# Five gated-state buffers instead of four, and output-projection weights that are loaded once for each sequence

## The chip, the cores and the metric

The kernel runs on one core of a Trainium2 chip. The metric is the device time of one execution in microseconds (us). Engines are named as in the profile: PE (TensorE), with PEld for its weight loads, DVE (VectorE), ACT (ScalarE), POOL (GpSimd) and SP (SyncE, which issues most DMAs). Each engine works through its own queue in order, and waits on semaphores for the others.

## The reference

The input is 16 sequences of 512 rows of 256 numbers, float32. A first layer is a Mamba block that scans in both directions, a second one is a soft mixture of experts; each ends with a sum and a layer norm.

```python
# layer 1, for each sequence
xf, res = split(x @ in_proj_w.T)                  # 512 channels each
xf = silu(causal_conv(xf));  xb = silu(causal_conv_b(xf))
delta = softplus(dt_proj(x_proj(xf)));  B, C = x_proj(xf)[...]   # 16 states
dA = delta * A;  dBu = delta * u * B              # for each channel, row and state
y = sum over states of C * (decayed running sum of dBu)  + u * D
y = (y_forward + y_backward) * silu(res)
x = layernorm(x + y @ out_proj_w.T)
# layer 2
x2 = layernorm(x) * gain + shift
logits = x2 @ slot_embeds.T                       # 16 experts x 64 slots
slots = softmax over rows(logits).T @ x2
e_out = (gelu(slots @ Wg + bg) * (slots @ Wu + bu)) @ Wd + bd
x = layernorm(x + softmax over slots(logits) @ e_out)
```

## The kernel before

**The scan.** For each of the 16 sequences `scan_part` runs four times: forward and backward for channels 0 to 255 (two chunks of 128), then both for channels 256 to 511. One call goes over the 16 states in pairs, and for each pair over its two chunks. A pair of states of one chunk is called a unit here: 64 units for each sequence, 1024 in all. What one unit does, with the lines of before:

- SP loads the rows of B and C for the pair, spread over all partitions, into `bs` (L431) and `cs` (L432), three buffers each, and sometimes a block of diagonals `dg` (L435).
- POOL makes `db`, the inputs of the recurrence, as `du` times `bs` (L442; 128x1024, three buffers).
- ACT makes the decay with an Exp, into the PSUM bank in which the scan will run (L459; three banks), and the gate `th` with a Tanh (L461; three buffers).
- DVE runs the recurrence (L465 forward, L467 backward; 128x512, twice in a unit) and multiplies it with the gate, (th + 1) * h, into one half of `hg` (L470, twice in a unit). `hg` is 128x1024, 4 KB for each partition, and has four buffers.
- POOL multiplies `hg` with `cs` in place (L471).
- PE adds `hg` up in the PSUM bank `acc`, by transposing it block by block against the identity (L386, eight matmuls of 128x128 for a unit). Only then is the `hg` buffer free.

For some states the product of L442 is made on PE instead, with diagonals, as `hd` (L420); its scan runs in that bank.

The matmuls of L386 are not issued with their unit. A unit is put on a list, and the list is worked off to a depth of two:

```python
pending.append((r == n == 0, n == 0, r == 1 and n == NS - 2, c, hg, accs, w, v["u"], f"acc_{q}_{c}", done))
evict()
...
beside_scan()
...
add_up(2)
```

So the sums of unit i stand in PE's queue behind what was issued beside units i + 1 and i + 2.

**The work beside it.** Everything else is written as generators that yield at places where they would wait: `prep` (input projections, convolutions, time steps for the next part), `front` (`finish`: output projection, norm, and then `dispatch`: logits and slots) and `back` (`experts` and `combine`, from sequence 3 on after each second one). `beside_scan` lets each give one piece after each unit. Instructions marked `late` keep their place in the program's order; for the others the builder's scheduler sets the order on each engine, by its own idea of times and of free buffers.

**finish and its weights.** `constants` loads the output projection's weights `outT` once, 128 x 4 x 256 float32, and halves them on DVE (L181, L182). `finish(b, y)` loads x again (L115), transposes y (L640), copies the transposed bank to `yt` on ACT (L645), multiplies with `outT` (L651, `po`), adds x (L660), norms, stores, makes the normed rows `xn`, and turns them into `x2T` (L691), one buffer of 4 KB for each partition. `x2T` goes to DRAM (L696) and is read by `dispatch` in the logits' matmuls (L710). `finish` of one sequence begins beside the first units of the next one, when `dispatch` of the sequence before has been drained.

**The end.** After the last scan the last sequence's `finish` and the last pair's experts and combine run with wider buffers.

Of the kernel before, what the change touches and what calls it, by code (L numbers as in the profile page):

```python
# [9 lines left out]
F32 = mybir.dt.float32  # L10
BF16 = mybir.dt.bfloat16
AF = mybir.ActivationFunctionType
ALU = mybir.AluOpType
# [4 lines left out]
P = 128  # L18
L = 512
NL = L // P  # L20
DM = 256
NM = DM // P
DI = 512
ND = DI // P
# [31 lines left out]
def seq_layers(tc, ident, neghalf, a, out):  # L56
# [22 lines left out]
    with ExitStack() as ctx:  # L79
# [47 lines left out]
        def late(ins):  # L127

            return tc.keep_in_program_order(ins)
# [45 lines left out]
        def constants():  # L175
            blanks(1)
            steps(side[0], "f", "")
            projections(side[1], "b", "_b")
            steps(side[1], "b", "_b")
            outT = const.tile([P, ND, DM], F32, name="outT")  # L180
            nc.sync.dma_start(outT, a["out_projT"].rearrange("(c p) o -> p c o", p=P))  # L181
            late(nc.vector.tensor_scalar(outT, outT, 0.5, None, ALU.mult))  # L182
            return outT

        projections(side[0], "f", "")
        blank = p2.tile([P, 4 * DM], F32, tag="W", name="blank", bufs=3)
# [220 lines left out]
        def scan_part(b, r, p, v, accs, done, then):  # L407
# [17 lines left out]
            for n in range(0, NS, 2):  # L425
                q = f"{b}_{r}_{p}_{n}"
                k = 1 if n + 1 in ds else 2

                bs = p4.tile([P, 2, L], F32, tag="bs", name=f"bs_{q}")
                cs = p4.tile([P, 2, L], F32, tag="cs", name=f"cs_{q}")  # L430
                nc.sync.dma_start(bs[:, :k, :], v["bc"][0, n : n + k, :].unsqueeze(0).to_broadcast([P, k, L]))  # L431
                nc.sync.dma_start(cs, v["bc"][1, n : n + 2, :].unsqueeze(0).to_broadcast([P, 2, L]))  # L432
                if n + 3 in ds:
                    dg = p4.tile([P, L], F32, tag="dg", name=f"dg_{q}", bufs=1)
                    nc.sync.dma_start(  # L435
                        dg.rearrange("p (l s) -> p l s", l=NL),
                        diag_dram[r, ds.index(n + 3), :, : P * P].rearrange("l (p s) -> p l s", p=P),
                    )
                for c in chunks:
                    dt, rr, du = v[c][:3]  # L440
                    db = p4.tile([P, 2, L], F32, tag="db", name=f"db_{q}_{c}")
                    nc.gpsimd.tensor_tensor(  # L442
                        db[:, :k, :], du.unsqueeze(1).to_broadcast([P, k, L]), bs[:, :k, :], ALU.mult
                    )
                    hg = p4.tile([P, 2, L], F32, tag="hg", name=f"hg_{q}_{c}", bufs=4)
                    hs = {}
                    for j in range(2):
                        if j < k:
                            dec = h = ps_h.tile([P, L], F32, tag="h", name=f"h_{q}_{c}_{j}")
                            hs[j] = (h, dec, db[:, j, :])  # L450
                        else:
                            h = made.pop((n + j, c))
                            dec = p4.tile([P, L], F32, tag="dec", name=f"dec_{q}_{c}", bufs=2)
                            hs[j] = (h, dec, h)

                    ths = {}
                    for j in range(2) if k == 2 else (1, 0):
                        s = slice(n + j, n + j + 1)
                        nc.scalar.activation(hs[j][1], dt, AF.Exp, scale=w["A"][:, c, s])  # L459
                        ths[j] = p4.tile([P, L], F32, tag="th", name=f"th_{q}_{c}_{j}")  # L460
                        nc.scalar.activation(ths[j], rr, AF.Tanh, bias=LN_1E12 / 2, scale=w["Ah"][:, c, s])  # L461
                    for j in range(2):
                        (h, dec, add), th = hs[j], ths[j]
                        if r == 0:
                            nc.vector.tensor_tensor_scan(h, dec, add, 0.0, ALU.mult, ALU.add)  # L465
                        else:
                            nc.vector.tensor_tensor_scan(  # L467
                                h[:, ::-1], dec[:, ::-1], add[:, ::-1], 0.0, ALU.mult, ALU.add
                            )
                        nc.vector.scalar_tensor_tensor(hg[:, j, :], th, 1.0, h, ALU.add, ALU.mult)  # L470
                    nc.gpsimd.tensor_tensor(hg, hg, cs, ALU.mult)  # L471
                    pending.append(
                        (r == n == 0, n == 0, r == 1 and n == NS - 2, c, hg, accs, w, v["u"], f"acc_{q}_{c}", done)
                    )
                    evict()

                    nxt_n = n if c == chunks[0] else n + 2
                    if nxt_n + 1 in ds:
                        for x in sides:
                            x.take_up()  # L480
                        by_diagonal(nxt_n + 1, chunks[1] if c == chunks[0] else chunks[0])
                    beside_scan()
                    if k == 1:
                        diags.pop(0)
                    add_up(2)
# [145 lines left out]
        def finish(b, y):  # L631

            xt = load_x(b)
            for h in range(NL // 2):
                yts = []
                for lc in (2 * h, 2 * h + 1):
                    yield 1
                    pt = bank(f"pyt_{b}_{lc}")
                    for c in range(ND):
                        nc.tensor.transpose(  # L640
                            pt[:, c * P : (c + 1) * P], y[:, c, lc * P : (lc + 1) * P], ident
                        )
                    yield HOLD
                    yt = p2.tile([P, L], F32, tag="fr", name=f"yt_{b}_{lc}")
                    late(nc.scalar.copy(yt, pt))  # L645
                    yts.append(yt)
                yield GAP + 1
                po = bank(f"po_{b}_{h}")
                for i, yt in enumerate(yts):
                    for c in range(ND):  # L650
                        nc.tensor.matmul(  # L651
                            po[:, i * DM : (i + 1) * DM],
                            yt[:, c * P : (c + 1) * P],
                            outT[:, c, :],
                            start=(c == 0),
                            stop=(c == ND - 1),
                        )
                yield HOLD
                x2 = xt[:, 2 * h : 2 * h + 2, :].rearrange("p c d -> p (c d)")
                late(nc.vector.tensor_tensor(x2, x2, po, ALU.add))  # L660
            mv = row_moments(nc, p2, xt, "m1", late)
            yield WAIT
            rs, sh = factors(mv, "m1")

            r2 = p2.tile([P, NL], F32, tag="m1_r2", name=f"m1_r2_{b}")
            nc.gpsimd.tensor_tensor(r2, mv[:, :, 1], rs, ALU.mult)
            nc.gpsimd.tensor_tensor(r2, r2, rs, ALU.mult)
            nc.gpsimd.tensor_scalar(r2, r2, EPS, None, ALU.add)
            nc.gpsimd.tensor_tensor(r2, r2, neghalf[:, :NL], ALU.pow)
            yield WAIT  # L670
            yield WAIT
            scaled(xt, xt, sh, rs)
            nc.scalar.dma_start(x1_dram[b].rearrange("(c p) d -> p c d", p=P), xt)
            yield 0
            xn = p1.tile([P, NL, DM], F32, tag="xn", name=f"xn_{b}")
            for i in range(NL):
                ins = nc.scalar.activation(xn[:, i, :], xt[:, i, :], AF.Identity, scale=r2[:, i : i + 1])
                if i == 0:
                    late(ins)
            yield WAIT  # L680
            x2T = p1.tile([P, NM, L], F32, tag="x2T", name=f"x2T_{b}")
            for k in range(NM):
                yield GAP + 1
                pt = bank(f"px2_{b}_{k}")
                for lc in range(NL):
                    nc.tensor.transpose(
                        pt[:, lc * P : (lc + 1) * P], xn[:, lc, k * P : (k + 1) * P], ident
                    )
                yield HOLD
                late(  # L690
                    nc.scalar.activation(  # L691
                        x2T[:, k, :], pt, AF.Identity, bias=shift[:, k : k + 1], scale=gain[:, k : k + 1]
                    )
                )
            if not wide:
                nc.scalar.dma_start(x2_dram[b].rearrange("k p l -> p k l"), x2T)  # L696
            yield from dispatch(b, xn, x2T)
# [341 lines left out]
        fwd = {}  # L1039
        prep.add(1, prep_forward(0, 0, ND, fwd))  # L1040
        prep.drain()
        outT = constants()
        prep.add(1, prep_pair(0, 0, 0, fwd))
        prep.drain()
        for w, s in zip(side, "fb"):
# [101 lines left out]
```

## Time and profile before

| | before |
|---|---|
| median of 3 runs | 5327.67 us (5324.82 to 5328.87) |
| the profiled execution | 5322.25 us, span 5320.5 us |
| PE busy | 4310.4 us (81%) |
| DVE busy | 4560.6 us (86%) |
| ACT busy | 4104.9 us (77%) |
| POOL busy | 4681.6 us (88%) |
| granted TensorE clock | 0.897 |
| DMA | 907.82 MB, mean 171 GB/s |

Busy time is the time in which an engine ran instructions of the program; the span is from the first to the last. A group in the profile is one kind of instruction: line, engine, operation, the tiles written and read, shapes and count; behind the bar its busy time, the mean of one in ns, and the engine's idle time just before these instructions with what ended most of it. A row of waits names who waited, for whom, total us, times and the longest.

### The profile page before, as it was taken

The numbers are of one execution on the slowest core, as the hardware profiler recorded it, in microseconds if no ns is written. First come the engines' busy times: TensorE is split into PE (matmuls) and PEld (weight loads), VectorE is DVE, ScalarE is ACT, GpSimd is POOL, SyncE is SP. The second block draws the span as 40 slices with busy tenths as digits, with TensorE's granted clock in tenths as the row PEclk, the third lists the DMA queues.
The fourth block names the chain that finished last, engine by engine and source line by source line (L and its number), as shares of the span: only waits on it lengthen the run. The fifth ranks groups of instructions, "written<-read, shape, count | busy, mean of one in ns | idle before, by whom it ended". The sixth has DMA issues, their size and how long they took to land. (4 is left out here: it accounts for less than half of the span.)

```text
span 5320.5 us, 74550 instructions
## 1 busy us (share of the span) xinstructions
PE 4310.4 (81%) x24498; PEld 3411.1 (64%) x24498; DVE 4560.6 (86%) x6284; ACT 4104.9 (77%) x6573; POOL 4681.6 (88%) x2537
## 2 busy tenths in 40 slices
PE   5677776897778978788788878889787897878889
PEld 3556565676567756676666766667666676657667
DVE  7999999889998899888898888988898889987733
ACT  6777878887888877888887887888778887777644
POOL 6999999989999899999999989998999989988710
PEclk7778888998899989999899988899888998889999
DMA  5444444675446644576446754467544664447545
GB/s 141 137 129 152 126 142 131 211 234 152 146 146 224 222 144 143 171 226 206 132 140 198 236 169 151 134 210 230 157 151 144 217 227 149 144 153 230 168 135 168
DMA packets 614820, 907.82 MB, mean 171 GB/s; under 512 B 84606, under 2 KB 404734, under 8 KB 614432
## 3 DMA queue, kind: packets, MB, share of 16 engines
q1 hardware_dynamic: 532740, 859.35, 50.9%
q10 hardware_dynamic: 81692, 43.70, 3.1%
q8 instruction: 195, 3.19, 0.2%
q14 instruction: 193, 1.58, 0.1%
HBM read 840.34 MB, written 62.56 MB: 170 GB/s over the span
## 5 line engine op out<-in xcount | busy, mean ns | idle before, releaser
L471 POOL TENSOR_TENSOR hg<-hg,cs 128x1024 f32<-128x1024 f32 x1024 | 2416.9, 2364 | 125.0 <-DVE hg L470 108.0
L442 POOL TENSOR_TENSOR db<-du,bs 128x1024 f32<-128x1024 f32 (+1 forms) x1024 | 2087.7, 2042 | 227.8 <-DVE h L465 84.1
L470 DVE SCALAR_TENSOR_TENSOR hg<-th,h 128x512 f32<-128x512 f32 x1744 | 1156.8, 679 | 183.4 <-PE acc L386 105.9
L386 PE MATMUL acc<-ident,hg 128*128 128x128 f32 x8192 | 1163.6, 292 | 106.4 <-POOL hg L471 84.6
L386 PEld LDWEIGHTS acc<-ident,hg 128*128 128x128 f32 x8192 | 1034.4, 152 | 284.6 <-POOL hg L471 131.3
L467 DVE TENSOR_TENSOR_SCAN h<-h,db 128x512 f32<-128x512 f32 x872 | 1044.9, 1219 | 104.9 <-ACT h L459 92.6
L465 DVE TENSOR_TENSOR_SCAN h<-h,db 128x512 f32<-128x512 f32 x872 | 1044.1, 1219 | 44.5 <-ACT h L459 43.6
L461 ACT ACTIVATE th<-rr,Ah_f 128x512 f32<-128x512 f32 x1024 | 724.6, 714 | 200.9 <-DVE hg L470 198.1
L461 ACT ACTIVATE th<-rr,Ah_b 128x512 f32<-128x512 f32 x1024 | 721.3, 712 | 153.5 <-DVE hg L470 143.5
L459 ACT ACTIVATE h<-dt,A_f 128x512 f32<-128x512 f32 x872 | 591.4, 680 | 99.5 <-DVE hg L470 96.3
L459 ACT ACTIVATE h<-dt,A_b 128x512 f32<-128x512 f32 x872 | 592.3, 680 | 85.6 <-DVE hg L470 81.7
L420 PE MATMUL hd<-dg,duT 128*128 128x128 f32 x2432 | 375.7, 305 | 73.2 <-ACT duT L364 27.1
L420 PEld LDWEIGHTS hd<-dg,duT 128*128 128x128 f32 x2432 | 347.9, 220 | 84.5 <-ACT duT L364 29.5
L710 PE MATMUL pl<-x2T,seT 128*128 128x512 f32 x512 | 294.1, 704 | 78.4 <-DVE hg L470 37.4
L838 PE MATMUL peo<-Wd,ht 128*128 128x256 f32 x1024 | 258.1, 408 | 63.2 <-DVE rr L346 36.6
L869 PEld LDWEIGHTS pg<-st,Wg 128*128 128x128 f32 x2048 | 243.1, 195 | 94.1 <-issue 82.8
L811 PE MATMUL pu<-st,Wu 128*128 128x128 f32 x2048 | 255.6, 284 | 49.3 <-DMA Wu<-in_Wu_dram 27.0
L1015 PE MATMUL cpo<-ceo,ct 128*128 128x256 f32 x1024 | 256.0, 407 | 43.2 <-DVE rr L346 40.0
L811 PEld LDWEIGHTS pu<-st,Wu 128*128 128x128 f32 x2048 | 245.9, 199 | 60.6 <-DVE h L467 29.5
L838 PEld LDWEIGHTS peo<-Wd,ht 128*128 128x128 f32 x1024 | 205.5, 206 | 106.1 <-DVE rr L346 39.2
L869 PE MATMUL pg<-st,Wg 128*128 128x128 f32 x2048 | 265.0, 284 | 4.5 <-DMA st<-s_dram 3.4
L1015 PEld LDWEIGHTS cpo<-ceo,ct 128*128 128x128 f32 x1024 | 207.2, 207 | 87.2 <-DVE rr L346 42.7
(165 smaller groups left out, 6754.0 us busy)
## 6 DMA issues: line engine op xcount, KB each, us to landing
cs<-bc SPq DMA_DIRECT2D x512, 512.0 KB, 3.9
bs<-bc SPq DMA_DIRECT2D x360, 512.0 KB, 5.2
Wg<-in_Wg_dram SPq DMA_DIRECT2D x128, 512.0 KB, 5.7
Wu<-in_Wu_dram SPq DMA_DIRECT2D x128, 512.0 KB, 5.8
Wd<-in_Wd_dram SPq DMA_DIRECT2D x128, 512.0 KB, 5.5
dg<-diag_dram SPq DMA_DIRECT2D x152, 256.0 KB, 4.3
bs<-bc SPq DMA_DIRECT2D x152, 256.0 KB, 3.5
x<-in_x_dram SPq DMA_DIRECT2D x32, 512.0 KB, 6.5
```

The lines of the kernel that those rows point to most:

```text
L386: ins = nc.tensor.matmul(accs[c][:, s], hc[:, j, s], ident, is_transpose=True, start=False, stop=(last and j == 1 and lc == NL - 1),)
L420: ins = nc.tensor.matmul(h[:, s], v[c][3][:, s], dg[:, s], start=True, stop=True)
L442: nc.gpsimd.tensor_tensor(db[:, :k, :], du.unsqueeze(1).to_broadcast([P, k, L]), bs[:, :k, :], ALU.mult)
L459: nc.scalar.activation(hs[j][1], dt, AF.Exp, scale=w["A"][:, c, s])
L461: nc.scalar.activation(ths[j], rr, AF.Tanh, bias=LN_1E12 / 2, scale=w["Ah"][:, c, s])
L465: nc.vector.tensor_tensor_scan(h, dec, add, 0.0, ALU.mult, ALU.add)
L467: nc.vector.tensor_tensor_scan(h[:, ::-1], dec[:, ::-1], add[:, ::-1], 0.0, ALU.mult, ALU.add)
L470: nc.vector.scalar_tensor_tensor(hg[:, j, :], th, 1.0, h, ALU.add, ALU.mult)
L471: nc.gpsimd.tensor_tensor(hg, hg, cs, ALU.mult)
L811: nc.tensor.matmul(pu[:, fc * P : (fc + 1) * P], got["Wu", e][:, k, fc * P : (fc + 1) * P], st[:, k, :, j * SL : (j + 1) * SL], start=(k = ...
L838: nc.tensor.matmul(po[:, j * DM : (j + 1) * DM], ht[:, fc, :], got["Wd", e0 + j][:, fc, :], start=(fc == 0), stop=(fc == NF - 1),)
L869: nc.tensor.matmul(pg[:, fc * P : (fc + 1) * P], got["Wg", e][:, k, fc * P : (fc + 1) * P], st[:, k, :, j * SL : (j + 1) * SL], start=(not ...
```

## The change

`hg` gets a fifth buffer. To make room, `outT` is no longer a constant of its own: each `finish` loads it again, into the buffer of `x2T`, which is of the same size. There it takes the place of the sequence before's turned rows, and it is overwritten by its own sequence's. The weights come unhalved, so the factor 0.5 moves into the eviction of the transposed y: the copy becomes an Identity activation with a scale of 0.5.

```diff
@@ constants()
-            outT = const.tile([P, ND, DM], F32, name="outT")
-            nc.sync.dma_start(outT, a["out_projT"].rearrange("(c p) o -> p c o", p=P))
-            late(nc.vector.tensor_scalar(outT, outT, 0.5, None, ALU.mult))
-            return outT
@@ scan_part
-                    hg = p4.tile([P, 2, L], F32, tag="hg", name=f"hg_{q}_{c}", bufs=4)
+                    hg = p4.tile([P, 2, L], F32, tag="hg", name=f"hg_{q}_{c}", bufs=5)
@@ finish(b, y)
             xt = load_x(b)
+            outT = p1.tile([P, ND, DM], F32, tag="x2T", name=f"outT_{b}")
+            nc.sync.dma_start(outT, a["out_projT"].rearrange("(c p) o -> p c o", p=P))
             for h in range(NL // 2):
...
-                    late(nc.scalar.copy(yt, pt))
+                    late(nc.scalar.activation(yt, pt, AF.Identity, scale=0.5))
@@ at the start
-        outT = constants()
+        constants()
```

## The prediction

> **What bounds the kernel now.** I first cut the span at 46 and 5080 us, the first `db` product and the last scan product, and asked for busy time in the two stretches.
>
> ```profile
> core 0: us, PE busy (x) PEld busy (x) DVE busy (x) ACT busy (x) POOL busy (x), PEclk, DMA share, GB/s
> 46.00:5080.00 5034.00, 4071.57 (x23243) 3225.50 (x23244) 4472.82 (x6051) 3993.91 (x6345) 4662.82 (x2478) 0.89 0.54 171
> ```
>
> The scans take 5034 of 5320.5 us. POOL works 4662.8 of them, 92.6%, and is idle 371; DVE works 88.9%. The other 240 us after 5080 have no `hg` in them. So POOL is the nearest to a bound, and the change can win at most its 371 idle us. The costliest groups show what POOL does:
>
> ```profile
> L471 POOL TENSOR_TENSOR hg<-hg,cs 128x1024 f32<-128x1024 f32 x1024 | 2416.9, 2364 | 125.0 <-DVE hg L470 108.0
> L442 POOL TENSOR_TENSOR db<-du,bs 128x1024 f32<-128x1024 f32 (+1 forms) x1024 | 2087.7, 2042 | 227.8 <-DVE h L465 84.1
> ```
>
> Each unit costs POOL 2.36 + 2.04 = 4.4 us, and what it waits for, when it waits, is DVE. Next, who DVE waits for, from the list of waits (total us, times, longest):
>
> ```profile
> ACT th L461 <- DVE hg L470: 341.6, 310, 3.2
> ...
> POOL hg L471 <- DVE hg L470: 108.0, 59, 7.8
> DVE hg L470 <- PE acc L386: 105.9, 89, 4.8
> ...
> DVE hd L467 <- PE hd L420: 40.6, 42, 1.9
> ...
> DVE hg L470 <- ACT th L461: 39.4, 33, 4.5
> ```
>
> The third line is the one that the change aims at: a gate (L470) wants a new `hg`, and the matmuls at L386 that read its old content four units ago have not run. 89 times, never over 4.8 us, about one unit's time (5034 us / 1024 units = 4.9 us). The timeline shows why they are late, and who pays:
>
> ```profile
> 3096.43 2.05 PE L869 MATMUL pg<-st,Wg 128*128 128x128 f32 x16
> ...
> 3098.32 1.04 PE L386 MATMUL acc<-ident,hg 128*128 128x128 f32 x8
> ...
> 3099.39 1.29 DVE L470 SCALAR_TENSOR_TENSOR hg<-th,h 128x512 f32<-128x512 f32 x2 [2.37 <-PE acc L386]
> ...
> 3100.82 2.35 POOL L471 TENSOR_TENSOR hg<-hg,cs 128x1024 f32<-128x1024 f32 x1 [2.61 <-DVE hg L470]
> ```
>
> L386 stands behind an expert's matmuls in PE's queue; DVE loses 2.37 us and POOL, which wants this very `hg` next, 2.61. At 85 of the 89 waits the gate was of the unit that POOL takes next: there is no store to live on.
>
> **Part 1: the fifth `hg`.** With five buffers a gate needs the matmuls of five units ago, one unit (4.9 us) earlier than now. The longest wait is 4.8 us, so all 105.9 us should go from DVE. What of it comes back in the span is another question. I went along the timeline and took, for each of the 89 waits, POOL's idle time within its next four instructions, at most the wait itself. Sequence 9 (of 0 to 15) as an example (wait, counted): 2.31, 1.69; 1.16, 0.93; 0.77, 0.77; 0.18, 0; 0.97, 0.97; 1.73, 0; 1.42, 0.69; 1.38, 1.38; 0.18, 0.18; 2.37, 2.37; 0.38, 0: 9.0 of 12.8 us. Over all sequences 71.2 of 105.9, a share of 0.67. Odd sequences from 3 to 13 hold most (7.2 to 9.0 each), the last has 15.6, the even ones from 4 on nothing.
>
> What is late next is PE itself: its queue is unchanged, and the diagonal product (L420) stands in it too. DVE waits for `hd` within 15 us behind these waits; taking each at most at the wait before it, that is 27.4 us. A DVE that comes earlier waits there again: 27.4 x 0.67 = 18.4 us are lost. 71.2 - 18.4 = 52.8 us of gain. Bounds: 0 (all comes back as another wait) to 105.9 (all of it is on the path). I take 52.8, from the waits themselves.
>
> **Part 2: the order.** Set side by side, the two programs have the same order on PE but for one transpose; about 1165 of DVE's 6285 instructions and 1080 of ACT's 6481 stand elsewhere, since the builder's order went by four buffers. 280 gates that had two or more instructions between them and their scan now have at most one; 147 went the other way. On POOL all but some 180 are in place. Gates nearer to their scans give POOL its input earlier, which is in my favour; but they may come before their `th`. Bounds: a gain of the 108 us that POOL waits for gates, most of them counted above already, and a loss of the 64 us worked out for the first rival below. I take 0, as the moves go both ways. ACT gets 351 table loads in place of 346, since five more pairs of the experts' Gelu are split by an Exp or Tanh. The groups have them at 1283 ns: 6.4 us of ACT, which is idle 1040 us of the scan stretch, but the loads stand in just the places where DVE is short. Bounds 0 to 6.4; I take 6.4.
>
> The page "ScalarE: Activation LUTs" of the Trainium skill, section "What ACT_TABLE_LOAD costs", speaks harder against this: a switch costs the load and a drain, together 2.66 us. By it this item would be an estimated 13.3 us. The trace shows no such drain: at 3058.89 a load of 1.28 us follows 0.02 us after an activation's end, and the next activation starts at 3060.19.
>
> **Part 3: the weights, once for each sequence.** Removed at the start: one DVE multiplication of 0.689 us at 38 us, while the first scan waits for its decay; 0. Added: 15 more DMAs of 0.5 MB (7.9 MB on 907.82), each 0.506 us to issue on SP, 7.6 us of SP in all, and 3.7 us to land. Each stands in SP's order near the second or third `bs` load of the next sequence and waits for the last L710 of the sequence before, which read `x2T`. SP at the place, in the timeline of before:
>
> ```profile
> 2773.55 0.32 SPq L431 DMA_DIRECT2D bs<-bc  x1
> 2783.65 0.32 SPq L432 DMA_DIRECT2D cs<-bc  x1
> 2785.96 0.32 SPq L431 DMA_DIRECT2D bs<-bc  x1
> 2786.37 0.39 SPq L435 DMA_DIRECT2D dg<-diag_dram  x1
> ```
>
> The last L710 before it ended at 2783.3. So the new load goes out at about 2783.7, and the `bs` and `dg` loads behind it, which went at 2786.0 and 2786.4, keep their time. They have more cover: from a `bs` issue to the product that reads it pass 22 us in the median, and 5.2 of those are the landing; from this `dg` to its matmul pass 24.2. `po`, the first reader of the weights, starts at 2839.6. The last sequence's load waits for an L710 that ended at 5049.4, and `po` starts at 5095.1. All hidden: 0. If the cover were gone, 15 x (0.506 + 3.7) = 63 us is the most the loads themselves could cost. The halving moves into the eviction (L645): a copy of 581 ns becomes an Identity with a constant scale. The nearest row is L274, PSUM in, 128x512, constant scale: 580 ns; the dearest is L691 with two per-row operands, 768. 64 x 0 to 64 x 0.187 = 0 to 12 us of ACT; I take 0, for L274.
>
> A rule that speaks against more loading is in "SBUF — State Buffer", section "A bandwidth-pool intuition that's wrong (but worth ruling out)": "HBM is almost always your end-to-end bottleneck". Were it so here, 7.9 MB at 170 GB/s would add an estimated 46 us and nearly undo the gain. The profile has the DMA engines at a share of 0.54 in the scan stretch, so no.
>
> **Sum.** 52.8 - 6.4 = 46 us. The profiled execution took 5322.25 us (span 5320.5), 0.1% under the median of 5327.67; I take the 46 us off the median: 5281 us, 0.9% faster. This case has its own range of 5222 (all 106 us) to 5317.
>
> **Rivals.**
> *The tanh takes the place of the buffer (slower).* Gates now stand nearer to their scans, so they may come before their `th`. Net 280 - 147 = 133 gates; each can wait for at most one Tanh, 0.714 us (L461): 95 us of DVE, by the same share of 0.67, 64 us. Against the gain of 46 that is 18 us slower, 5346. It decides from 46 / (0.714 x 0.67) = 96 of the 133 gates. For it: DVE waits for `th` already, 39.4 us. Against it: only 33 times, though 401 gates follow their scan directly today, and ACT waits 341.6 us for DVE to free a `th`, so ACT is mostly early.
> *PE is the bound at these places (no change).* The fifth buffer is there but the next thing from PE (`hd`, `pl`, `pz`) comes no earlier. For it: PE's queue has the same order and is 81% busy, and 27.4 us of `hd` waits do follow. Against: 62 us in all on `hd`, against 106. Time: 5328 - 0 to 10.
> *SP is blocked (slower).* If L710 is later in the changed run, `bs`, `cs` and `dg` stand behind the weights' load. It costs nothing until the delay is over some 15 us; then each us counts in 15 places, 5 us too many make 75, and with the gain 5357. Against: the margin above.
>
> **How the numbers follow.** Forecast 0.68; tanh 0.16; PE 0.10; SP 0.06. The three runs of before lie within 0.08%, so I call anything within 0.2% (10.7 us) no change. The PE case and a little of the neighbours make 0.10 of no change; tanh and SP make 0.22 slower. The range goes from 5222, the full 106 us, to 5350, just over the tanh case. SP's case and a gain beyond 106 through the better order stay outside.
>
> **What would show it.** The wait of L470 on L386 should fall from 106 us to under 10, POOL's idle time in the scan stretch from 371 to about 325, and its L471 waits on L470 from 108 to about 70. Waits of DVE on `hd` should grow from 62 towards 80. Wrong if the wait of L470 on `th` goes from 39 to near 100 (tanh), if L386's wait goes but POOL's idle stays at 371 (PE), or if POOL waits for the landing of `bs` (SP).

## The result, and the profile after

The changed kernel is slower: 5362.94 us (5356.56 to 5378.82) against 5327.72, ratio 1.0071 with an interval of 1.0047 to 1.0096. The profiled execution took 5368.21 us, span 5366.4, at a granted clock of 0.894 (before 0.897). Before was timed anew beside each batch of the experiments, with medians from 5327.5 to 5329.3 us. Times are medians of fast runs; one of the eleven runs of `rows_moved` came in the slower state (5423.51 us) and is left out. The scans end at 5124 us in place of 5080; the tail is 242.6 us, before 240.4. The lines of this kernel up to `finish` stand four lower than before: the gate is L466, the product of POOL L467, `db` L438, the scans L461 and L463, Exp L455, Tanh L457, the sums L382, `hd` L416, the scaled rows of a norm L621.

The scan stretch, and the two groups of POOL:

```profile
core 0: us, PE busy (x) PEld busy (x) DVE busy (x) ACT busy (x) POOL busy (x), PEclk, DMA share, GB/s
46.00:5130.00 5084.00, 4106.05 (x23269) 3241.34 (x23270) 4459.40 (x6051) 4000.20 (x6349) 4660.31 (x2478) 0.89 0.54 171
```

```profile
L467 POOL TENSOR_TENSOR hg<-hg,cs 128x1024 f32<-128x1024 f32 x1024 | 2414.5, 2361 | 112.6 <-DVE hg L466 44.0
L438 POOL TENSOR_TENSOR db<-du,bs 128x1024 f32<-128x1024 f32 (+1 forms) x1024 | 2084.8, 2039 | 284.0 <-issue 114.0
```

POOL doesn't work longer than before: 4660 us in the stretch, before 4663. DVE and ACT are within 15 us of before; PE, at the slightly lower clock, is busy 4341.6 us of the whole execution, before 4310.4. The difference on POOL is idle time; taken from 44.6 to 5123.8 us it goes from 371 to 417. `hg` waits less for its input (125.0 to 112.6), `db` more (227.8 to 284.0); 44 of these 56 us stand under "issue" (70.2 to 114.0), for which the profile names no releaser. The list of waits says for what (total us, times, longest):

```profile
ACT th L457 <- DVE hg L466: 359.9, 348, 8.5
...
DVE h L463 <- ACT h L455: 125.2, 57, 5.9
...
ACT x L621 <- POOL m_sh L616: 85.1, 16, 7.7
...
DVE hg L466 <- PE acc L382: 77.1, 45, 6.1
...
DVE hg L466 <- ACT th L457: 46.5, 41, 6.0
...
POOL hg L467 <- DVE hg L466: 44.0, 42, 6.4
```

The gate's wait for the sums, at which the buffer aimed, is 77.1 us and not gone (before 105.9). At each of its 45 places the missing sum is that of the unit five before, where it was four before: VectorE now runs one unit further ahead and finds the fifth buffer taken too. The scans wait longer for the Exp (backward 92.6 to 125.2), and a wait that was at 42.6 us has doubled: ScalarE's scaled rows of the output norm, for POOL's factors. The timeline shows one such place, in sequence 8:

```profile
2587.61 0.60 ACT L621 ACTIVATE x<-x,m_sh,m_rs 128x256 f32<-128x256 f32 x1 [7.68 <-POOL m_sh L616]
...
2588.12 0.67 ACT L455 ACTIVATE h<-dt,A_b 128x512 f32<-128x512 f32 x1
...
2588.82 1.23 DVE L463 TENSOR_TENSOR_SCAN h<-h,db 128x512 f32<-128x512 f32 x1 [5.86 <-ACT h L455]
...
2589.36 6.77 PE L1015 MATMUL cpo<-ceo,ct 128*128 128x256 f32 x16 [6.22 <-ACT duT L360]
...
2596.17 0.48 DVE L1024 SCALAR_TENSOR_TENSOR cx<-cpo,csm,cx 128x256 f32<-128x256 f32 x1 [4.94 <-PE cpo L1015]
...
2600.47 2.36 POOL L438 TENSOR_TENSOR db<-du,bs 128x1024 f32<-128x1024 f32 x1 [5.43 <-DVE h L463]
```

Only the first row of a norm is `late`; the other three are free, and the builder has put one of them in front of Exps and copies. ScalarE stands at it for 7.68 us, and what is queued behind it is late: an Exp, for which the scan waits 5.86 us, and two copies of `duT`, for which TensorE waits 6.22 us before it makes `cpo` (a product of `combine`). VectorE then waits 4.94 us for `cpo`, the scans behind that are late too, and POOL, which needs a buffer that a scan reads, pays 5.43. Before, the copies ran ahead of the rows, and the four rows ran together at this place, with next to no wait:

```profile
2578.41 2.08 ACT L625 ACTIVATE x<-x,m_sh,m_rs 128x256 f32<-128x256 f32 x4 [0.45 <-POOL m_sh L620]
```

In after one row stands five places ahead of the next in twelve sequences (2 to 13); in before two or three places in eight of the sixteen.

### The profile page after: what moved, and what is told of

Same layout as the page of the kernel before. It is cut to its first block, busy times and chain, and to the rows that moved or that the text cites. A ratio compares the mean times of both kernels' runs of the same rounds, so it can differ in the third digit from the quotient of the medians.

```text
span 5366.4 us, 74363 instructions
## 1 busy us (share of the span) xinstructions
PE 4341.6 (81%) x24498; PEld 3422.9 (64%) x24498; DVE 4548.0 (85%) x6283; ACT 4111.5 (77%) x6578; POOL 4680.4 (87%) x2537
## 4 chain that ended last, share of the span: by engine, by line
DVE 38%; PE 28%; ACT 16%; issue 11%; POOL 5%; DMA 2%; SPq 0%; DVEq 0%; ACTq 0%; POOLq 0%
DVE h L463 10%; DVE hg L466 9%; DVE h L461 9%; PE acc L382 4%; ACT th L457 4%; ACT h L455 3%; PE peo L838 3%; PE pl L710 2%; PE pg L869 2%; PE cpo L1015 2%; PE px L287 2%; POOL db L438 2%; POOL hg L467 2%; PE pq L746 2%; PE hd L416 2%
## 5 line engine op out<-in xcount | busy, mean ns | idle before, releaser
L467 POOL TENSOR_TENSOR hg<-hg,cs 128x1024 f32<-128x1024 f32 x1024 | 2414.5, 2361 | 112.6 <-DVE hg L466 44.0
L438 POOL TENSOR_TENSOR db<-du,bs 128x1024 f32<-128x1024 f32 (+1 forms) x1024 | 2084.8, 2039 | 284.0 <-issue 114.0
L466 DVE SCALAR_TENSOR_TENSOR hg<-th,h 128x512 f32<-128x512 f32 x1744 | 1155.7, 677 | 164.5 <-PE acc L382 77.1
L382 PE MATMUL acc<-ident,hg 128*128 128x128 f32 x8192 | 1164.5, 292 | 119.8 <-POOL hg L467 96.4
L382 PEld LDWEIGHTS acc<-ident,hg 128*128 128x128 f32 x8192 | 1033.6, 152 | 298.1 <-POOL hg L467 130.2
L463 DVE TENSOR_TENSOR_SCAN h<-h,db 128x512 f32<-128x512 f32 x872 | 1044.3, 1218 | 134.2 <-ACT h L455 125.2
L461 DVE TENSOR_TENSOR_SCAN h<-h,db 128x512 f32<-128x512 f32 x872 | 1046.7, 1218 | 66.5 <-ACT h L455 60.6
L457 ACT ACTIVATE th<-rr,Ah_f 128x512 f32<-128x512 f32 x1024 | 724.1, 714 | 219.5 <-DVE hg L466 216.7
L457 ACT ACTIVATE th<-rr,Ah_b 128x512 f32<-128x512 f32 x1024 | 723.4, 712 | 146.9 <-DVE hg L466 143.2
L455 ACT ACTIVATE h<-dt,A_f 128x512 f32<-128x512 f32 x872 | 592.0, 681 | 110.1 <-DVE hg L466 104.0
L455 ACT ACTIVATE h<-dt,A_b 128x512 f32<-128x512 f32 x872 | 591.2, 679 | 77.7 <-DVE hg L466 75.1
L416 PE MATMUL hd<-dg,duT 128*128 128x128 f32 x2432 | 368.3, 301 | 64.0 <-ACT duT L360 29.5
L416 PEld LDWEIGHTS hd<-dg,duT 128*128 128x128 f32 x2432 | 338.3, 215 | 75.8 <-ACT duT L360 31.6
L1015 PE MATMUL cpo<-ceo,ct 128*128 128x256 f32 x1024 | 264.2, 417 | 79.3 <-DVE rr L342 39.4
L869 PEld LDWEIGHTS pg<-st,Wg 128*128 128x128 f32 x2048 | 256.7, 204 | 98.1 <-issue 82.8
L869 PE MATMUL pg<-st,Wg 128*128 128x128 f32 x2048 | 278.9, 293 | 5.3 <-DMA st<-s_dram 3.5
```

Of the source, the lines that this page charges most:

```text
L382: ins = nc.tensor.matmul(accs[c][:, s], hc[:, j, s], ident, is_transpose=True, start=False, stop=(last and j == 1 and lc == NL - 1),)
L416: ins = nc.tensor.matmul(h[:, s], v[c][3][:, s], dg[:, s], start=True, stop=True)
L438: nc.gpsimd.tensor_tensor(db[:, :k, :], du.unsqueeze(1).to_broadcast([P, k, L]), bs[:, :k, :], ALU.mult)
L463: nc.vector.tensor_tensor_scan(h[:, ::-1], dec[:, ::-1], add[:, ::-1], 0.0, ALU.mult, ALU.add)
L869: nc.tensor.matmul(pg[:, fc * P : (fc + 1) * P], got["Wg", e][:, k, fc * P : (fc + 1) * P], st[:, k, :, j * SL : (j + 1) * SL], start=(not ...
L1015: nc.tensor.matmul(po[:, :DM], cts[sc // 4][:, sc % 4 * P : (sc % 4 + 1) * P], eos[sc // 4][:, sc % 4, :], start=(sc == 0), stop=(sc == NS ...
```

## The experiments

Orders are held with edges between neighbours on an engine that carry no semaphore; the matmuls, data and buffers stay as they are (shortened here):

```python
for engine, steps in want.items():        # the other program's order
    for i in steps:
        tc.add_manual_dep(i, prev.name, NoSync, reason="order"); prev = i
```

**1. The three parts of the change: weights, buffer, order.** `weights_only` has four buffers:

```diff
-  hg = p4.tile([P, 2, L], F32, tag="hg", name=f"hg_{q}_{c}", bufs=5)
+  hg = p4.tile([P, 2, L], F32, tag="hg", name=f"hg_{q}_{c}", bufs=4)
```

> The weights' part of the change alone: they are loaded for each sequence and halved in the eviction, with four gated-state buffers; the order on PE, DVE, POOL is that of before (DVE within 4 of 6285 instructions). Theory A (the fifth buffer is good by itself, but the builder's order, which counts with it, puts waiting instructions in front of the scan's on ACT, DVE and POOL): the weights cost nothing, 5323 to 5333 us. Theory B (the reload through SP's queue and the new activation are the loss): 5350 to 5365 us. Theory C (the fifth buffer is of no use, PE sets the pace at those places, and the new order is the whole loss): 5323 to 5333 us as in A.

5333.09 us, ratio 1.0012 (1.0003 to 1.0021). `five_old_order` has five, with the order of before held on all five engines:

> The whole change, but with the order of before pinned on all five engines (the 16 loads of the weights stand free on SP). Theory A: the gain of the prediction appears, 5270 to 5300 us, and the wait of the gates for the sums falls from 106 to under 20 us. Theory B: the gain less the loss by the reload, 5310 to 5340 us. Theory C: 5322 to 5334 us, the waits for the sums turned into others.

5324.68 us, ratio 0.9993 (0.9984 to 1.0002). So the weights cost 5.6 us, the buffer under one order gives 8.4, and the builder's new order costs 5362.9 - 5324.7 = 38 us. By the spread of the runs I estimate that the first two are good to some 3 us, and every difference from after to some 10, as its four runs lie 22 us apart. The granted clock doesn't explain the 38: the run of after at 0.899 took 5357.68 us, those of `five_old_order` at 0.898 from 5315.89 to 5326.81. `five_old_order` lies in theory C's range and not in A's, and as C says, the waits for the sums turned into others. The buffer does what it says: in `five_old_order` no wait of the gate for the sums is left in the list (95.5 us in `weights_only`). What the list has in its place:

```profile
DVE h L463 <- ACT h L455: 128.0, 97, 3.4
...
DVE hd L463 <- PE hd L416: 58.0, 49, 4.4
DVE hg L466 <- ACT th L457: 56.6, 41, 6.0
...
DVE h L461 <- ACT h L455: 44.1, 32, 3.5
DVE hd L461 <- PE hd L416: 39.5, 26, 4.6
```

Against `weights_only` the Exp's waits are up by 24 us (147.7 to 172.1), those for `hd` by 42 (55.1 to 97.5), for Tanh by 12 (44.8 to 56.6): 78.6 of 95.5 us came back on the same engine.

**2. Which engine's order.** The same kernel with ScalarE's order alone held, and with VectorE's alone:

> The whole change with the order of before pinned on ACT alone; the builder then leaves DVE within 600 and POOL within 70 instructions of the order of before. Theory A, if ACT's early norm (the scaled rows that wait 7.7 us for POOL ahead of the scan's Exp) is the main loss: 5280 to 5325 us, and the wait of the scaled rows for POOL falls from 85 to about 43 us. If DVE's order is: 5340 to 5365 us. Theory B: 5345 to 5365 us. Theory C: 5328 to 5350 us.

> The whole change with the order of before pinned on DVE alone; POOL and PE then come out as before, and ACT within 50 instructions, with 12 more table loads than before (15 us of ACT). Theory A: 5280 to 5315 us. Theory B: 5325 to 5355 us. Theory C: 5328 to 5343 us.

5360.82 (1.0048 to 1.0073) and 5353.99 us (1.0039 to 1.0064). Neither mends it: they are 36 and 29 us above `five_old_order`. With ScalarE's order held the even sequences from 4 on no longer lose, but the odd ones do, 3 to 7 us each; with VectorE's held, the builder splits more pairs of Gelus (358 table loads), and most odd sequences lose 3 to 5 us. One engine's order without the others' is no repair. In `five_old_act` ScalarE has the rows and the 346 table loads of before, so what is wrong with ScalarE's order in after isn't needed for a loss of this size.

**3. The early rows.** One line, so that no scaled row can leave its place:

```diff
-                if i == 0:
-                    late(ins)
+                late(ins)
```

> The changed kernel with one line moved: all four scaled rows of a norm are kept in program order on ScalarE, and not the first alone, so that no row can be put ahead of the Exps and copies of the scan. The weights and the five buffers stay. Theory (the new order loses where a scaled row that the builder put early waits for GpSimd's norm factors with ScalarE's queue behind it): the 4.1 us that each even sequence loses at unit 19 goes, 25 us over six even sequences, 12 more table loads or fewer make no difference, so 5363 - 25 = 5338 us (5330 to 5346), and ScalarE's wait for the norm factors falls from 85 us in 16 waits to under 50. The odd sequences keep their 3.5 to 5 us each. Rival (the new order is worse everywhere, and this place is only where a lag that is already there shows): the loss goes to the next wait, 5355 to 5370 us, with the even sequences still behind by 4 to 6 us each.

5297.48 us, ratio 0.9939 (0.9925 to 0.9952): 65 us off, more than either theory gave. But this builds a new order, with some 400 of VectorE's instructions elsewhere, so the row was then moved alone, in after and in before, all else held:

> The changed kernel with its own order held on all five engines, and twelve instructions of ScalarE moved: in sequences 2 to 13 the one scaled row of the output norm that stands four instructions ahead of the others is put right before them. Nothing else moves, and the 351 table loads stay. Theory (most of the loss is this one row, since with all rows kept in order the kernel takes 5297 us): 12 rows that wait some 5 us each with ScalarE's queue behind them are about 50 us, so 5363 - 50 = 5313 us (5300 to 5330), and ScalarE's wait for the norm factors falls from 85 to under 50 us. Rival (the row costs only the 4.1 us of unit 19 in even sequences, and the rest of that kernel's gain came from the other instructions that moved with it, 400 of VectorE's 6285 and twelve table loads less): 5363 - 25 = 5338 us (5332 to 5345).

> The kernel before with its order held on all five engines, and the first scaled row of the output norm put next to the second in the eight sequences in which it stands two or three places ahead (in the others it stands in its place). Theory (before pays for the row in each second sequence, 3.6 us at unit 19 in six of them, and after in both kinds): 5328 - 22 = 5306 us, 5298 to 5312; then after's early rows cost 29 us against 22, and only 7 of the 35 us between the kernels are theirs. Rival (before's row is free, and its 31 us came from the hundred other instructions that moved): 5322 to 5330 us; then all 29 us of after's rows are new.

After: 5332.35 us (ratio to before 1.0007, 0.9998 to 1.0016), 31 us for twelve rows, which is just in the rival's range. Before: 5310.21 us, ratio 0.9969 (0.9959 to 0.9979), 19 us for eight, as its theory says. So before paid for its early rows as well, at unit 19 of its odd sequences, and only 12 of the 35 us between the two kernels are theirs. The line itself, in before and with four buffers:

> The kernel before, four buffers and its weights loaded once, with all scaled rows of a norm kept in program order. Theory (before, too, waits for the norm factors, 64.8 and 42.6 us, but without much behind it, as its row stands two or three places ahead and not five): 5329 us, 5318 to 5332, no difference. Rival (the line is worth its 65 us with four buffers too, and the fifth buffer has no part in it): 5265 to 5300 us.

> The changed kernel with four buffers and all scaled rows in program order: beside the run with five it gives what the fifth buffer is worth once the early row is gone. Theory (weights cost 5 us, the buffer is worth about 35 us with an order in which no row waits): 5334 us, 5322 to 5338. Rival (the rows' order is the gain, with any number of buffers): within 8 us of the 5297 us with five.

5297.49 (0.9932 to 0.9958) and 5298.47 us (0.993 to 0.9958). The rivals of both held: the 31 us have nothing to do with the fifth buffer, and beside 5297.48 for five the buffer is worth 1 us once the builder orders for itself. Weights loaded sixteen times cost 1.0 us here. Neither of these can be told from zero: five runs each lie 10 to 16 us apart. The line also holds the rows of `combine`'s norm, whose wait for their factors falls from 64.8 to 48.6 us in before; what that part gives alone wasn't tried.

**4. A pair that the new order splits.** One pass of `experts` has 16 Gelus, one for each expert, in pairs; such a pass is called a group of Gelus here. In after, ScalarE's seventh and eighth Gelu of a group have an Exp between them:

```profile
2968.30 1.28 ACT L892 ACT_TABLE_LOAD   x1
2969.59 0.60 ACT L892 ACTIVATE ht<-pg 128x512 f32<-128x512 f32 x1
...
2970.82 1.28 ACT L455 ACT_TABLE_LOAD   x1
2972.11 0.69 ACT L455 ACTIVATE h<-dt,A_f 128x512 f32<-128x512 f32 x1
...
2972.82 1.28 ACT L895 ACT_TABLE_LOAD   x1
2974.12 0.60 ACT L895 ACTIVATE ht<-pg 128x512 f32<-128x512 f32 x1
...
2975.82 1.28 ACT L455 ACT_TABLE_LOAD   x1
2977.11 0.69 ACT L455 ACTIVATE h<-dt,A_f 128x512 f32<-128x512 f32 x1
```

Before, the same two stand together behind one load:

```profile
2961.99 0.60 ACT L892 ACTIVATE ht<-pg 128x512 f32<-128x512 f32 x1
2962.48 0.59 ACT L895 ACTIVATE ht<-pg 128x512 f32<-128x512 f32 x1
```

Four loads, of which two go when the pair stands together. With the rows moved and these six pairs joined (351 loads become 339):

> The run with twelve rows moved (5334 us), and beside that the experts' seventh and eighth Gelu, which the new order alone has apart with an Exp between them, put together in six groups: 12 table loads of 1.28 us less, nothing else moved. Theory (what is left of the loss is this split pair; after's sequences lose 3.6 us at the unit where it stands): 5334 - 20 = 5314 us (5308 to 5322), ahead of before by 0.3%. Rival (the pair is hidden; the rest is VectorE's order): 5328 to 5336 us.

5322.82 us, ratio 0.9990 (0.9981 to 0.9999): 10 us off, for 12 loads of 1.28 us or 15.4. In its list of waits the rows' wait is back near before's, and the gate's wait for the sums is as large as in after:

```profile
DVE hg L466 <- PE acc L382: 75.5, 44, 5.6
...
ACT x L621 <- POOL m_sh L616: 49.6, 15, 8.3
```

Two more pairs of each group changed with the order: the last one has a load between its Gelus in after (at 3118.44 and 3122.35 us) and none in before (3097.01 and 3098.52), and with the third pair it is the other way round. They weren't tried singly.

**5. What the buffer is worth under one order, without early rows.** Five buffers, held in the order that `four_rows_late` came out with:

> The changed kernel with five buffers, held on all five engines in the order that four buffers with all rows in order came out with (5298 us). Theory (under one order the buffer is worth what it was worth before, 8 us): 5290 us, 5284 to 5296. Rival (once no row stalls ScalarE the buffer's waits are real, and it is worth 25 us or more): 5275 or less. The other rival (no worth at all): 5297 to 5301.

5283.68 us, ratio 0.9915 (0.9901 to 0.9929), 14.8 less than the 5298.47 with four buffers. The gate's wait for the sums is gone again (114.0 with four), and again most of it stands elsewhere:

```profile
DVE h L463 <- ACT h L455: 129.0, 97, 4.9
...
DVE hg L466 <- ACT th L457: 57.2, 37, 4.4
DVE hd L463 <- PE hd L416: 52.6, 46, 4.4
...
ACT x L621 <- POOL m_sh L616: 17.9, 15, 3.6
```

With four buffers these four rows have 97.8, 40.2, 42.5 and 15.0 us. The builder's own order for five buffers (5297.48) gives these 14 us away again. On which engine was asked by holding one at a time:

> The changed kernel with five buffers and all scaled rows in order; VectorE alone is held in the order that four buffers came out with, and the builder orders the rest for itself. TensorE and GpSimd come out as in the 5283.7 us run, ScalarE with 52 of 6476 instructions elsewhere and 12 table loads more (358). Theory (the 14 us lie in VectorE's order): 5284 + 12 x 1.28 x 0.5 = 5291 us at most, 5282 to 5293. Rival (they lie in ScalarE's, where Gelus are split): 5298 us or more.

> The same with ScalarE alone held, in the order of the 5283.7 us run. TensorE comes out the same, VectorE with 570 of 6285 instructions elsewhere, GpSimd with 70. Theory (VectorE's order): 5294 to 5302 us, as without the hold. Rival (ScalarE's): 5280 to 5288.

5315.39 (0.9960 to 0.9983) and 5322.82 us (0.9981 to 0.9998), both worse than holding all or none. The first lies in its rival's range (ScalarE's order), the second in neither's. The first differs from the run of 5283.68 us by 52 of ScalarE's instructions and 12 table loads, 15.4 us, and by 13 loads of `cs` on SP, which isn't held; it loses 32. `five_old_dve` stands to `five_old_order` in the same way: TensorE, VectorE and GpSimd have the same order, some 50 of ScalarE's instructions and 14 of SP's stand elsewhere, ScalarE has 12 loads more (358 to 346), and 29 us are lost. So a small change in ScalarE's order is enough for some 30 us, twice the loads' own time; which of its instructions does it wasn't tried. Since ScalarE's good order alone doesn't keep the gain either, an order is one thing over all engines.

**6. What the buffer runs into.** Gelu computed as Tanh, so that ScalarE changes no table around it, with four and with five buffers in the order of before:

> Four buffers, the weights loaded for each sequence, the order of the kernel before on all five engines, and the experts' Gelu computed as Tanh (another function, so other numbers come out), which needs no change of table around it: 192 table loads in place of 346. It is the base for the next run. 154 loads of 1.28 us are 198 us of ScalarE's time. If ScalarE's pair of Gelus with its loads sets the pace in the expert steps, this alone is worth 50 us or more: 5333 - 50 = 5283 us or less. If TensorE and GpSimd set it, 5315 to 5333 us.

> The same with five buffers. Theory (the fifth buffer's 95 us of waits came back at once as waits for ScalarE, because the Gelus and their table loads hold its queue): with the loads gone the buffer is worth 25 us or more against the run with four. Rival (TensorE, or GpSimd's own work, is right behind, so that no freed engine helps): the gap stays at 8 us, between 0 and 14.

5279.83 (0.9894 to 0.9921) and 5240.21 us (0.9820 to 0.9847). The buffer is worth 39.6 us here, and POOL is idle 284 us. So ScalarE's table loads at the experts' Gelus held back most of these 39.6 us. TensorE has a share too: of the 125.9 us that the gate waits for the sums with four buffers, 70 still come back, as waits for the Exp (29 us more), for `hd`, which TensorE makes (26), and for Tanh (15). Joining all split pairs keeps Gelu as it is:

> The changed kernel with all scaled rows in order (5297 us), its order then held on all engines, and each experts' Gelu that has an Exp or Tanh between it and its pair moved behind that, next to the second: 339 table loads become 305, 34 of 1.28 us or 43.6 us of ScalarE. Theory (in the expert steps ScalarE's loads set the pace, as Tanh in Gelu's place showed: 40 us between four and five buffers, and 84 us with five): half of it or more reaches the end, 5297 - 25 = 5272 us, 5255 to 5285. Rival (the first Gelu of a pair now comes later, and what waits for it takes the place): 5290 to 5305 us.

> The same, and all 27 pairs of Gelus put together: 310 table loads in place of 346, 46 us of ScalarE. Theory (the loads hide the buffer, so fewer of them show more of it): 5290 - 30 = 5260 us, 5250 to 5270, the fastest of all. Rival (the first Gelu of a pair comes later and holds up the experts): 5285 or more.

5276.96 (0.9891 to 0.9919), 20.5 us below the same order with split pairs, and 5279.93 us (0.9893 to 0.9920), 3.8 below, which four runs each, 9 to 11 us apart, can't tell from nothing. 43.6 and 46.2 us of ScalarE went; in the second order ScalarE merely idles more (1003 to 1053 us). The two can't be told apart, and are the fastest versions with Gelu: 1.6% under after, 0.95% under before.

**7. The new order early, the old one later.** After's own order for sequences 0 to 3, where it was 6.9 us ahead, and that of before from there:

> The changed kernel with the order of before held on all five engines from the fifth sequence on; in the first four the builder orders for itself. Theory (the buffer gains a little and the builder's order loses it from the fifth sequence on; in the first four the new order was 6.9 us ahead of before, and the old one with five buffers 6.3 us behind): 5324.7 - 13 = 5312 us, 5306 to 5320, faster than before by 0.3%. Rival (what is gained early is lost again, since a later wait is for a step that doesn't come sooner): 5322 to 5330 us, no difference from before.

5310.88 us, ratio 0.9968 (0.9956 to 0.9981): what is won early is kept.

## Why the prediction was wrong

The forecast of 5281 us, faster, failed: the change made the kernel slower, 5363 us. The steps, with what the runs gave:

| term of the sum | predicted | measured |
|---|---|---|
| fifth buffer, same order | -52.8 | -8.4 (early rows as before), -14.8 (rows in order) |
| the new order | 0 and 6.4 for loads | +38, or +14 with rows in order |
| weights | 0 | +5.6, or +1.0 with rows in order |

**The step that decided the sign is Part 2, "I take 0, as the moves go both ways".** It counted gates nearer to or farther from their scans, and looked at no other instruction among the 1080 that move on ScalarE. Its outer bound, +64, came from the Tanh. The 38 us are a difference of orders. Early rows cost 31 us in after and 19 in before, +12; one more split pair of Gelus in each of six groups costs 10; and 17 are left that moving single instructions didn't find. This division is an estimate: it takes the 19 us of before over to five buffers, where these rows weren't moved, and it has after's uncertainty of some 10 us. What the runs show directly is that after with rows and pairs mended takes 5322.82 us, as much as the order of before with five buffers (5324.68), which still has eight early rows. After's order still waits 75.5 us for the sums there, where the old order with five buffers waits for none, so I take the rest to lie in how the engines' orders fit each other; that isn't shown, and which instructions do it stays open.

The row could have been seen ahead. The order of the changed program has it, five places ahead of its fellows against three, two or none in before, and before's list of waits had the price: "ACT x L625 <- POOL m_sh L620: 42.6, 15, 6.2", up to 6.2 us at one instruction with ScalarE's queue behind it.

**Part 1** had the aim right and the size wrong. All 105.9 us "should go from DVE", and under one order they do. The term that was mis-sized is what is late next: 18.4 us for `hd` alone, where the Exp, `hd` and the Tanh took back 78.6 of 95.5. The share of 0.67, POOL's idle time behind each wait, said that POOL paid for these waits; it didn't say that POOL would be fed if they went. It reaches the end with 8.4 of 95.5, 0.09, or 14.8 of 114.0, 0.13. Only with ScalarE's loads out of the way does it become 39.6 of 125.9, 0.31. The larger part of the cause was in the sentence on loads, which "stand in just the places where DVE is short"; it was used for five new pairs and not for those that were there.

**The loads.** 6.4 us for five more loads had the right sort of price: six pairs, 12 loads, are worth 10 us at the end of 15.4 on the engine. But the five are a balance: in each of six groups two pairs are newly split and one is newly joined.

**Part 3.** No wait for the weights appears, as argued, and SP's rival is out: POOL waits 3.9 us for `bs` in after, 4.6 before. The 5.6 us of `weights_only` were put at nothing. Its profiled execution is 13 us longer than that of before, of which 6.7 come in the last three sequences and 3 in the tail (243.4 us against 240.4). With rows in order 1.0 us is left, within the noise. What passes them on wasn't tried. The eviction takes 592 ns in `weights_only`, not 580: 0.7 us over 64.

**The rivals.** Tanh's waits went from 39.4 to 46.5 us only, so the slower case had the direction by luck and the wrong mechanism. "PE is the bound" is half right. Under the order of before its sign appears: the wait for the sums is gone, POOL's idle time stays at 374 us (before 371, `weights_only` 382), 5324.68 us lies in its range, and `hd`, which PE makes, took back 42 of the 78.6 us. That PE isn't the only bound is what experiment 6 shows.

**What would show it.** The signs were of use: the gate's wait at 77 and not under 10 said that the fifth buffer was being spent under the new order. POOL's idle time of 336 us (forecast 325) came in `five_rows_order`, at 5283.68 us, where the forecast was 5281. That isn't the forecast's mechanism, though: 31 of its 44 us below before are what the line on the scaled rows gives by itself.

## What to carry to other kernels

Where a scheduler orders by its own idea of free buffers, one more buffer is a new program: compare it with the old order held, before saying what the buffer is worth, and read the new order for an instruction that now stands ahead of its input with a queue behind it. Such an instruction costs the queue's wait, not its own duration, and one line that keeps it in place was worth 31 us here without any buffer. An engine's wait that is taken away is worth what the next arrival leaves of it: with ScalarE, TensorE and POOL 77%, 81% and 88% busy, about a tenth.

## What the runs showed of the hardware

What table loads of 1.28 us were worth at the end went by the order that they stood in: 34 of them fewer gave 20.5 us of 43.6 in one order, 36 fewer 3.8 of 46.2 in another (within the noise), 12 fewer 10 of 15.4, and the 154 around Gelu (198 us) 84 with five buffers and 53 with four. POOL's costliest instruction, the product with `cs`, took the same time in every order (2361 to 2370 ns in all kernels), so the differences on POOL were waits.
